# Strassen's seven products for the queries of two heads, with the projection and the keys' transfers moved

## The chip, the core and the metric

The kernel runs on one core of a Trainium2 chip. The metric is device time in microseconds (us) of one launch; less is better. A core has TensorE (PE, matmul; its weight loads are listed as PEld), VectorE (DVE), ScalarE (ACT), GpSimd (POOL) and SyncE (SP), each with a queue of its own that it works off in order, and 16 DMA engines that move data between HBM and on-chip memory. Matmuls write to PSUM, in banks of 128 x 512 floats; the other operands are in SBUF.

## The reference, cut to what matters

All is float32. The input x is 4 batches of 512 rows and 512 columns; a context of 4 x 512 x 256 goes with it. Two layers follow one another; the change is in the second layer's attention, of 16 heads of 128.

```python
# layer 0: attention on the context and a linear map of 4-bit weights
x = x + tanh(g_xattn[0]) * L0_xattn(layernorm(x), ctx)
x = x + tanh(g_ffn[0]) * L0_ffn(layernorm(x))
# layer 1: cross attention, then 16 experts (4 of them for each row of the first batch's 512)
x = x + tanh(g_xattn[1]) * L1_xattn(layernorm(x), ctx)
x = x + tanh(g_ffn[1]) * L1_ffn(layernorm(x))

def L1_xattn(hidden, ctx):
    q = (hidden @ Wq).reshape(B, S, H, D)       # Wq 512 x 2048
    k = (ctx @ Wk).reshape(B, Skv, H, D)        # Wk 256 x 2048
    v = (ctx @ Wv).reshape(B, Skv, H, D)
    q, k = rmsnorm(q, gq), rmsnorm(k, gk)
    attn = softmax(einsum("bqhd,bkhd->bhqk", q, k) / sqrt(D))
    return einsum("bhqk,bkhd->bqhd", attn, v).reshape(B, S, H * D) @ Wo
```

## The kernel before

**Stages.** Layer 0 fills the first 200 us. Layer 1's attention then runs in 32 *groups* m, each one batch and one pair of heads; a group has two *steps* i = 2m + h, one for each head, and each step has four *quarters*, one for each 128 query rows. `step(i)` (L1026) says which pieces are emitted in which quarter. The order of all engines' work is written by hand: `later(n, f)` puts a piece off until n further 512-column matmuls have been emitted, and `tick()` counts one. Each engine gets its instructions in the order of emission, so a piece that is emitted earlier stands ahead of the others on that engine's queue.

**One group.** For group m+1, `keys_values` (8 matmuls of 512 columns, L586) fills keys and values in steps h = 0; ScalarE copies them out of PSUM (L580, L581). The keys are squared (L601), summed on VectorE (L605), scaled on POOL by their inverse root mean square (rk L173, then kn L612), turned in 32x32 blocks on VectorE (L623), and put into the layout of the scores by a round trip to HBM on ScalarE's queue: one transfer out (k_d) and four back (kT, L638), all four at once.

`queries(m+1, h)` runs at h = 1, one head in each of the first two quarters: four matmuls of 512 columns (L660) into one PSUM bank, then ScalarE takes the squares (L666) and the scaled copy qT (L668) straight from PSUM. For both heads, VectorE sums the squares (part, L680), TensorE adds over partitions (L688), VectorE masks and scales (own, L693, and qss, L696), and POOL raises to the power −1/2 (rq, L173).

`scores(i, c)`, one in each quarter, is a matmul (L709) and then on VectorE the row maximum (nmax, L717) and its product with rq (sb, L719), on ScalarE the exponential with its sum (L722), and on VectorE the reciprocal (rden, L726), the division (prob, L727) and the turn of the blocks (tP, L243). With the last quarter `move_probs` issues 16 DMAs on SP (L251), which bring the turned blocks to where `values` needs them (the tile big). `values(i − 2)` is four matmuls (L749) into the single bank psO, copied out by ScalarE (oT, L756). `project` is eight matmuls of a group's two heads with Wo (L776), four pairs, each added to x on VectorE (L258); before the change two pairs run at h = 1 and the other two at the next group's h = 0, in the last quarter.

**Buffers.** PSUM has three banks psA (used by keys_values, queries, project and the experts in turn), two psS (scores), two psT, one psO. The queries' weights wq have two buffers and are loaded two groups ahead, at h = 1's last quarter; `sq` is one buffer that the keys' and the queries' squares share.

**Extra work in some groups.** In groups 11 to 27 (steps 22 to 55) blocks of the experts stand between the pieces (`block_work`, matmuls L853). Groups 4 and 5, 12 and 13, 20 and 21 also normalise and transpose the next batch's rows (`next_rows`), and groups 9 and 10 the rows for the experts (`moe_rows`). In steps 57 to 60 POOL gathers the experts' rows and VectorE adds them back (L258).

Of the kernel before, what the change touches and what calls it, by code (L numbers as in the profile page):

```python
# [9 lines left out]
F32 = mybir.dt.float32  # L10
# [5 lines left out]
P = 128  # L16
# [38 lines left out]
def tile_gated_decoder(  # L55
# [31 lines left out]
    def ps_a():  # L87
        return ps("psA", 3)
# [4 lines left out]
    def ps_t():  # L93
        return ps("psT", 2)
# [7 lines left out]
    def lnt():  # L102
        return work.tile([P, KC, S], F32, tag="lnT", bufs=2, name="lnT")

    def row(tag, bufs):
        return work.tile([P, 512], F32, tag=tag, bufs=bufs, name=tag)

    def col(n, tag):
        return tiny.tile([P, n], F32, tag=tag, name=tag)
# [15 lines left out]
    def load_x(b):  # L125
        nc.sync.dma_start(x_sb[:, b * NC : (b + 1) * NC, :], x_v[:, b * NC : (b + 1) * NC, :])

    wq0 = const.tile([P, CC, D], F32, name="wq0")
    nc.sync.dma_start(wq0, wq0_d.rearrange("(c p) d -> p c d", p=P))
    load_ctx(0)  # L130
    wk0 = const.tile([P, CC, D], F32, name="wk0")
    nc.sync.dma_start(wk0, wk0_d.rearrange("(c p) d -> p c d", p=P))
    small = const.tile([P, NSMALL], F32, name="small")
    nc.sync.dma_start(small, small_d)
# [51 lines left out]
        return mv, rs  # L186

    def normalised(b, c, mv, rs):
        xn = row("xn", 2)
        nc.vector.tensor_scalar(  # L190
            xn, x_sb[:, b * NC + c, :], mv[:, c, 0:1], rs[:, c : c + 1], ALU.subtract, ALU.mult
        )
        return xn
# [168 lines left out]
    def route():  # L362
        def small_tile(shape, tag, dtype=F32):
            return pool0.tile(shape, dtype, tag=tag, bufs=1, name=tag)
# [14 lines left out]
        partf = small_tile([P, 1], "partf")  # L379
        nc.vector.tensor_copy(partf, parti)  # L380

        zero = row("xg", 1)
        nc.gpsimd.memset(zero, 0.0)
        blank = y_d[(NE + SPILL) * P :, :].rearrange("(s p) d -> p s d", p=P)
        nc.gpsimd.dma_start(blank, zero.unsqueeze(1).broadcast_to([P, NSLOT - NE - SPILL, DM]))
# [5 lines left out]
        nc.vector.tensor_copy(idx, topi)  # L391
        idx_v = idx.rearrange("p (c k) -> p c k", k=TOPK)
        ef_b = ef.unsqueeze(1).broadcast_to(CE)
        hit = small_tile([P, TOPK, NC, NE], "hit")
        for k in range(TOPK):
            nc.vector.tensor_tensor(
                hit[:, k], ef_b, idx_v[:, :, k].unsqueeze(2).broadcast_to(CE), ALU.is_equal
# [100 lines left out]
    for c in range(KC):  # L498
        bb = tiny.tile([P, P], F32, tag="bb", bufs=2, name="bb")
        nc.vector.tensor_scalar(bb, ones, bcol[:, c : c + 1], None, ALU.mult)  # L500
        nc.tensor.matmul(pb[:, c * P : (c + 1) * P], bb, ident, start=True, stop=True)
    brow = row("y", 2)
    nc.vector.tensor_copy(brow, pb)

    def linear(b, lx, chunks):
# [22 lines left out]
    GD = G * D  # L528
    groups = [(b, g) for b in range(NB) for g in range(NG)]
    wq_of, wkv_of, wo_of = {}, {}, {}  # L530
    q_of, sq_of, rq_of, kn_of, k_of, v_of, o_of = {}, {}, {}, {}, {}, {}, {}
    turned, moved = {}, {}

    def cols(m):
        g = groups[m][1]
        return slice(g * GD, (g + 1) * GD)

    def load_wkv(m):
# [2 lines left out]
        nc.sync.dma_start(t[:, :, 1, :], wv_v[:, :, cols(m)])  # L541
        wkv_of[m] = t

    def load_wq(m):
        t = work.tile([P, KC, GD], F32, tag="wq", name="wq")
        nc.sync.dma_start(t, wq_v[:, :, cols(m)])
        wq_of[m] = t

    def load_wo(m):
        g = groups[m][1]  # L550
# [9 lines left out]
    def later(n, f):  # L560
        heapq.heappush(pending, (clock[0] + n, next(serial), f))

    def tick(n=1):
        if n == 0:
            return
        clock[0] += n
        while pending and pending[0][0] <= clock[0]:
            heapq.heappop(pending)[2]()

    def keys_values(m, chunks):  # L570
# [61 lines left out]
                st["tK"].rearrange("p j h c q -> p (j h c q)"),  # L632
            )

        def take_in():
            kT = work.tile([P, NT, G, P], F32, tag="kT", name="kT")
            for j in range(NT):
                nc.scalar.dma_start(  # L638
                    kT[j * TB : (j + 1) * TB].rearrange("r t h q -> r t (h q)"),
                    st["k_d"][:, :, j, :].rearrange("t r q -> r t q"),  # L640
                )
            k_of[m] = kT

        later(2, squares)
        later(4, scale)
        later(11, turn)
        later(14, put_out)
        later(18, take_in)

    def queries(m, h):  # L650


        b, wq = groups[m][0], wq_of[m]
        if h == 0:
            sq_of[m] = work.tile([P, G, S], F32, tag="sq", bufs=1, name="sq")
            q_of[m] = []
        sq = sq_of[m]
        pp = ps_a()
        for k in range(KC):
            nc.tensor.matmul(  # L660
                pp, wq[:, k, h * D : (h + 1) * D], lx1[b][:, k, :], start=(k == 0), stop=(k == KC - 1)
            )
            tick()

        def copies():
            nc.scalar.activation(sq[:, h, :], pp, AF.Square)  # L666
            qT = row("qT", 3)
            nc.scalar.activation(qT, pp, AF.Identity, scale=gqk)  # L668
            q_of[m].append(qT)

        later(1, copies)
        if h < G - 1:
            return
        n = G * S // TB
        st = {}

        def part():

            st["part"] = col(n, "part")
            nc.vector.tensor_reduce(  # L680
                st["part"], sq.rearrange("p h (j r) -> p (h j) r", r=TB), AX.X, ALU.add,
                apply_transpose=True,
            )

        def total():

            st["pq"] = ps_t()
            nc.tensor.matmul(st["pq"][:, 0:n], same, st["part"], start=True, stop=True)  # L688

        def scale():  # L690

            own = col(n, "own")
            nc.vector.tensor_tensor(own, st["pq"][:, 0:n], mine, ALU.mult)  # L693
            v = col(G * NC, "qss")
            nc.vector.tensor_reduce(v, own.rearrange("p (c a) -> p c a", a=NT), AX.X, ALU.add)
            nc.vector.tensor_scalar(v, v, 1.0 / D, EPS, ALU.mult, ALU.add)  # L696
            rq_of[m] = col(G * NC, "rq")
            rsqrt(rq_of[m], v, G * NC)

        later(2, part)  # L700
        later(8, total)
        later(9, scale)
# [81 lines left out]
    up_v = up_d.rearrange("e i n -> (e i) n")  # L784
    down_v = down_d.rearrange("e i n -> (e i) n")

    def moe_rows():

        stats = {}

        def chunk(c):
            xn = normalised(0, c, *stats[0])
            later(1, lambda: nc.sync.dma_start(xn_d[c * P : (c + 1) * P, :], xn))

        return [lambda: stats.update({0: layernorm_rows(0)})] + [
            lambda c=c: chunk(c) for c in range(NC)
        ]

    def gather(out, table, k, s):
        nc.gpsimd.indirect_dma_start(  # L800
# [149 lines left out]

    def next_rows(b):

        t = lnt()
        mv, rs = layernorm_rows(b)
        lx1[b] = t
        return [lambda c=c: rows_chunk(t, b, c, mv, rs) for c in range(NC)]

    def rows_chunk(t, b, c, mv, rs):
        xn = normalised(b, c, mv, rs)
        pt = ps_t()  # L960

        def turn():
            for k in range(KC):
                nc.tensor.transpose(pt[:, k * P : (k + 1) * P], xn[:, k * P : (k + 1) * P], ident)

        later(3, turn)
        later(4, lambda: nc.scalar.copy(
            t[:, :, c * P : (c + 1) * P], pt.rearrange("p (k q) -> p k q", k=KC)
        ))

    extra = {}

    def put(i, quarter, *fs):
        extra.setdefault((i, quarter), []).extend(fs)
# [5 lines left out]
    put(4, 3, lambda: load_down(order[0]))  # L980
    for j, f in enumerate(moe_rows()):
        put(first - 3 + j // 4, j % 4, f)
    put(first - 2, 3, lambda: load_rows(order[0]))
    for j, s in enumerate(order):
        for (i, quarter), fs in block_work(s, order[j + 1] if s != order[-1] else None).items():
            put(first + 2 * j + i, quarter, *fs)
# [3 lines left out]
            put(last + 1 + c, k, lambda c=c, k=k: add_row(c, k))  # L990
    for b in range(1, NB):
        i = (b - 1) * NG * G + NG
        chunks = []
        put(i, 3, lambda b=b, chunks=chunks: chunks.extend(next_rows(b)))
        for c in range(NC):
            put(i + 1 + c, 3, lambda c=c, chunks=chunks: chunks[c]())
        if b > 1:
            put(i, 3, lambda b=b: load_ctx(b))

# [1 line left out]


    n, M = G * len(groups), len(groups)
    lxs = [layernorm_T(b) for b in (NB - 2, NB - 1)]
    load_wkv(0)
    load_wq(0)
    load_wkv(1)
    load_wq(1)
    load_wo(0)
    load_wo(1)  # L1010
    keys_values(0, [0, 1, 2, 3])
# [2 lines left out]
    lx1[0] = layernorm_T(0)  # L1014
    keys_values(1, [0, 1, 2, 3])
    tick(30)
    queries(0, 0)
    queries(0, 1)
    tick(30)
    layer0.close()  # L1020
    moe = ctx.enter_context(tc.tile_pool(name="moe", bufs=1))
    for c in range(NC):
# [3 lines left out]
    def step(i):  # L1026
        m, h = divmod(i, G)
        pieces = [[], [], [], []]
        if i >= G:
            pieces[2].append(lambda: values(i - G))  # L1030
        elif h > 0:
            pieces[3].append(lambda: tick(8))
        if h == 0:
            if 0 < m < M - 1:
                pieces[0].append(lambda: keys_values(m + 1, [0, 1]))
                pieces[1].append(lambda: keys_values(m + 1, [2, 3]))
            if m + 2 < M:
                pieces[3].append(lambda: load_wkv(m + 2))
            if m >= 2:
                pieces[3].append(lambda: project(m - 2, [2, 3]))  # L1040
            if 2 <= m < M:
                pieces[3].append(lambda: later(4, lambda: load_wo(m)))
        else:
            if m + 1 < M:
                pieces[0].append(lambda: queries(m + 1, 0))
                pieces[1].append(lambda: queries(m + 1, 1))
            if m + 2 < M:
                pieces[3].append(lambda: load_wq(m + 2))
            if m >= 1:
                pieces[3].append(lambda: project(m - 1, [0, 1] if m < M else [0, 1, 2, 3]))  # L1050
        for quarter in range(4):
            if i < n:
                scores(i, quarter)
            for f in pieces[quarter] + extra.get((i, quarter), []):
                f()

    with tc.manual_schedule():
# [74 lines left out]
```

## Time and profile before

| what | us |
|---|---|
| median of 3 runs | 1508.68 (1507.06 to 1510.2) |
| the profiled execution, its own time | 1506.07 |
| its span, first to last instruction | 1504.3 |
| mean granted TensorE clock in it | 0.985 |
| first scores of group 0 | 211.0 |
| first scores of group 2 | 284.29 |
| first scores of group 11 (nine groups later) | 602.29 |
| first scores of groups 28, 29, 30 | 1330.21, 1374.26, 1411.71 |

The profile comes from one execution. In its rows an instruction is named by engine, line, operation and tiles ("nmax<-psS" reads psS and writes nmax), with its duration and, in brackets, the idle time of its engine just before it and what ended that. A matmul of 512 columns in float32 appears as two records, so a group's 40 matmuls are 80 records (and three small ones). Most of the page's costliest waits belong to engines that have less to do, and cost nothing by themselves:

```profile
L722 ACT ACTIVATE prob<-psS,sb,rq 128x512 f32<-128x512 f32 x256 | 199.2, 778 | 605.3 <-DVE sb L719 582.0
L717 DVE TENSOR_REDUCE nmax<-psS 128x1 f32<-128x512 f32 x256 | 173.0, 676 | 39.5 <-PE psS L709 37.6
L776 PE MATMUL psA<-wo,oT 128*128 128x512 f32 x512 | 238.6, 604 | 11.7 <-ACT oT L756 11.7
```

The first of these rows says that ScalarE's exponentials (256, of 778 ns) were preceded by 605 us of idle time, 582 of it ended by VectorE's sb; the second that VectorE's row maxima were preceded by 39.5 us, mostly ended by the scores' matmul; the third that TensorE waited 11.7 us in the whole run for oT.

### The profile page before, as it was taken

To read this page: it belongs to the slowest core of one execution; us is meant where nothing else is said; L and a number is where in the kernel's file an instruction comes from. 1 tells how busy PE (TensorE), PEld (TensorE's weight loads), DVE (VectorE), ACT (ScalarE), POOL (GpSimd) and SP (SyncE) were. 2 spreads that over 40 slices of the span, in tenths; PEclk is the share of its full clock that TensorE was granted. 3 is DMA by queue.
4 is the path that set the end of the run, shared out by engine and by line. 5 is a ranking of instruction groups with operands and counts; after the bars stand their busy time and mean duration, and the time that the engine had idled before them with its cause. 6 is when DMAs were issued, how large, how long until landed. Compare 5 with 4: busy or idle time off the path is not lost. (4 is left out here: it accounts for less than half of the span.)

```text
span 1504.3 us, 13711 instructions
## 1 busy us (share of the span) xinstructions
PE 1440.6 (96%) x3705; PEld 671.2 (45%) x3705; DVE 961.6 (64%) x2170; ACT 522.1 (35%) x1175; POOL 287.4 (19%) x210
## 2 busy tenths in 40 slices
PE   5899999899999999999999999999999999989987
PEld 2444444344444444444444444444444444434433
DVE  5875537577777777666565655566656655666783
ACT  3521224333343433333333333324333333333331
POOL 2434411221111111111101111112011111112210
PEclk8899999999999999999999999999999999999998
DMA  9610013554444546456665665556656655545643
GB/s 332 231 47 1 15 56 84 151 145 135 126 143 135 147 137 178 117 170 193 174 185 171 184 203 155 174 163 201 184 164 184 184 169 177 171 121 156 182 126 91
DMA packets 156114, 227.93 MB, mean 152 GB/s; under 512 B 24832, under 2 KB 90896, under 8 KB 156032
## 3 DMA queue, kind: packets, MB, share of 16 engines
q1 hardware_dynamic: 128080, 178.91, 40.8%
q10 hardware_dynamic: 23040, 33.56, 7.3%
q0 software_dynamic: 4912, 14.53, 3.4%
q8 instruction: 32, 0.52, 0.1%
q14 instruction: 50, 0.41, 0.1%
HBM read 129.62 MB, written 30.17 MB: 106 GB/s over the span
## 5 line engine op out<-in xcount | busy, mean ns | idle before, releaser
L722 ACT ACTIVATE prob<-psS,sb,rq 128x512 f32<-128x512 f32 x256 | 199.2, 778 | 605.3 <-DVE sb L719 582.0
L709 PE MATMUL psS<-kT,qT 128*128 128x512 f32 x512 | 263.1, 597 | 4.5 <-DMA big<-tP 2.5
L776 PE MATMUL psA<-wo,oT 128*128 128x512 f32 x512 | 238.6, 604 | 11.7 <-ACT oT L756 11.7
L660 PE MATMUL psA<-lnT,wq 128*128 128x512 f32 x512 | 232.9, 596 | 8.2 <-DVEq L894 7.6
L749 PE MATMUL psO<-big,v 128*128 128x512 f32 x512 | 232.8, 598 | 5.2 <-DMA big<-tP 5.2
L586 PE MATMUL psA<-wkv,ctx 128*128 128x512 f32 x512 | 233.5, 596 | 0.2 <-DVE x_sb L258 0.2
L717 DVE TENSOR_REDUCE nmax<-psS 128x1 f32<-128x512 f32 x256 | 173.0, 676 | 39.5 <-PE psS L709 37.6
L243 DVE STREAM_TRANSPOSE tP<-prob 128x512 f32<-128x512 f32 x256 | 181.9, 711 | 9.0 <-DVE prob L727 0.6
L726 DVE RECIPROCAL rden<-den 128x1 f32<-128x1 f32 x256 | 40.6, 159 | 224.6 <-ACT prob L722 219.0
L749 PEld LDWEIGHTS psO<-big,v 128*128 128x128 f32 x512 | 98.1, 192 | 129.6 <-issue 121.7
L776 PEld LDWEIGHTS psA<-wo,oT 128*128 128x128 f32 x512 | 96.9, 193 | 131.0 <-issue 105.4
L660 PEld LDWEIGHTS psA<-lnT,wq 128*128 128x128 f32 x512 | 97.2, 191 | 129.6 <-issue 107.6
L173 POOL TENSOR_TENSOR rq<-qss,mhalf 128x8 f32<-128x8 f32 x32 | 53.3, 1667 | 516.6 <-DVE qss L696 516.6
L258 DVE SCALAR_TENSOR_TENSOR x_sb<-psA,tg,x_sb 128x512 f32<-128x512 f32 x160 | 113.8, 728 | 57.6 <-PE psA L776 21.8
L586 PEld LDWEIGHTS psA<-wkv,ctx 128*128 128x128 f32 x512 | 96.8, 191 | 118.8 <-issue 106.5
L727 DVE TENSOR_SCALAR prob<-prob,rden 128x512 f32<-128x512 f32 x256 | 133.5, 521 | 9.0
L173 POOL TENSOR_TENSOR rk<-kss,mhalf 128x8 f32<-128x8 f32 x32 | 52.5, 1640 | 447.5 <-DVE rden L726 279.8
L709 PEld LDWEIGHTS psS<-kT,qT 128*128 128x128 f32 x512 | 93.2, 191 | 95.6 <-issue 73.2
L853 PE MATMUL psA<-gu,xgT 128*128 128x352 f32 x272 | 86.0, 459 | 0.0
L623 DVE STREAM_TRANSPOSE tK<-kn 128x256 f32<-128x256 f32 x128 | 45.5, 413 | 49.5 <-POOL kn L612 49.5
L853 PEld LDWEIGHTS psA<-gu,xgT 128*128 128x128 f32 x272 | 51.7, 190 | 37.9 <-issue 16.3
L756 ACT COPY oT<-psO 128x512 f32<-128x512 f32 x64 | 37.4, 585 | 77.4 <-PE psO L749 70.2
(157 smaller groups left out, 1283.7 us busy)
## 6 DMA issues: line engine op xcount, KB each, us to landing
big<-tP SPq DMA_DIRECT2D x1024, 64.0 KB
wq<-in_wq_dram SPq DMA_DIRECT2D x32, 512.0 KB
wo<-in_wo_dram SPq DMA_DIRECT2D x32, 512.0 KB
k_d<-tK ACTq DMA_DIRECT2D x32, 512.0 KB
kT<-k_d ACTq DMA_DIRECT2D x128, 128.0 KB
gu<-in_gate_dram SPq DMA_DIRECT2D x16, 704.0 KB
gu<-in_up_dram SPq DMA_DIRECT2D x16, 704.0 KB
wkv<-in_wk_dram SPq DMA_DIRECT2D x32, 256.0 KB
```

The lines of the kernel that those rows point to most:

```text
L173: nc.gpsimd.tensor_tensor(out, v, mhalf[:, :n], ALU.pow)
L243: nc.vector.transpose(tP[:, :, c, :], e.rearrange("p (j r) -> p j r", r=TB))
L258: nc.vector.scalar_tensor_tensor(x_sb[:, t, :], src, gate, x_sb[:, t, :], ALU.mult, ALU.add)
L586: nc.tensor.matmul(pp, ctxs[b][:, k, c * P : (c + 1) * P], wkv[:, k, :, :].rearrange("p a n -> p (a n)"), start=(k == 0), stop=(k == CC - 1),)
L660: nc.tensor.matmul(pp, wq[:, k, h * D : (h + 1) * D], lx1[b][:, k, :], start=(k == 0), stop=(k == KC - 1))
L709: nc.tensor.matmul(sc, q_of[m][h][:, c * P : (c + 1) * P], k_of[m][:, :, h, :], start=True, stop=True)
L717: nc.vector.tensor_reduce(nmax, sc, AX.X, ALU.max, negate=True)
L722: nc.scalar.activation(st["e"], sc, AF.Exp, bias=sb, scale=scale, accum_out=st["den"])
L727: nc.vector.tensor_scalar(st["e"], st["e"], rden, None, ALU.mult)
L749: nc.tensor.matmul(po, v[:, k, h * D : (h + 1) * D], pT[:, :, k, :], start=(k == 0), stop=(k == NC - 1))
L776: nc.tensor.matmul(pp, oT[:, j, c * P : (c + 1) * P], wo[:, j, :], start=(j == 0), stop=(j == G - 1))
L853: nc.tensor.matmul(st[a][:, :FF], st["xgT"][:, k * P : (k + 1) * P], st["gu"][:, a, k, :], start=(k == 0), stop=(k == KC - 1),)
```

## The change

**The queries' product.** For a group, the transposed queries of two heads are a 2 x 2 arrangement of quarters: head by half of the rows (256). Each was the sum of two products, over the halves of the 512 model columns, eight in all. Now there are seven products, by Strassen's scheme in Winograd's form, each two matmuls of 256 columns (14 a group instead of 8 of 512). The sums of quarters of the weights are made once a group on POOL (`combine`), those of the normalised rows once a batch on VectorE (`combine_rows`). The products' sums are made partly by accumulation in PSUM (the first product opens px[:, 0:256] and stays to be added to), partly by five `tensor_tensor` of 128x256 on VectorE and two copies on ScalarE. The squares and the scaled copies (in place) then read SBUF, all four after the last sum.

```diff
     def load_wq(m):
-        t = work.tile([P, KC, GD], F32, tag="wq", name="wq")
-        nc.sync.dma_start(t, wq_v[:, :, cols(m)])
-        wq_of[m] = t
+        w = work.tile([P, KC, GD], F32, tag="wq", bufs=1, name="wq")
+        nc.sync.dma_start(w, wq_v[:, :, cols(m)])
+        sums = work.tile([P, 3, HK, D], F32, tag="wqs", bufs=1, name="wqs")
...
+        def combine():
+            s1, s2, s4 = (sums[:, j] for j in range(3))
+            s3 = quarter(1, 0)
+            nc.gpsimd.tensor_tensor(s1, quarter(1, 0), quarter(1, 1), ALU.add)
+            nc.gpsimd.tensor_tensor(s2, s1, quarter(0, 0), ALU.subtract)
+            nc.gpsimd.tensor_tensor(s3, quarter(0, 0), s3, ALU.subtract)
+            nc.gpsimd.tensor_tensor(s4, quarter(0, 1), s2, ALU.subtract)
+            wq_of[m] = [quarter(0, 0), quarter(0, 1), s4, quarter(1, 1), s1, s2, s3]
+
+        return combine
+
+    def combine_rows(b):
...
+        nc.vector.tensor_tensor(t3, quarter(1, 1), quarter(0, 1), ALU.subtract)
+        nc.vector.tensor_tensor(t1, quarter(0, 1), quarter(0, 0), ALU.subtract)
+        nc.vector.tensor_tensor(t2, quarter(1, 1), t1, ALU.subtract)
+        nc.vector.tensor_tensor(t4, quarter(1, 0), t2, ALU.subtract)
+        lxs_of[b] = [quarter(0, 0), quarter(1, 0), quarter(1, 1), t4, t1, t2, t3]
...
+    def queries(m, part):
...
+        def product(j, out, start):
+            for k in range(HK):
+                nc.tensor.matmul(
+                    out, ws[j][:, k, :], xs[j][:, k, :], start=start and k == 0, stop=k == HK - 1,
+                    skip_group_check=True,
+                )
+                tick(0.5)
+
+        if part == 0:
+            px, py = ps_a(), ps_a()
...
+            def second():
+                nc.scalar.copy(u2, px[:, 0:HS])
+                nc.vector.tensor_tensor(u2, px[:, HS:S], u2, ALU.add)
+
+            def fourth():
+                nc.vector.tensor_tensor(u3, py[:, 0:HS], u2, ALU.add)
+                nc.vector.tensor_tensor(q1[:, HS:S], py[:, HS:S], u3, ALU.add)
+
+            product(0, px[:, 0:HS], True)
+            product(5, px[:, HS:S], False)
+            later(0, second)
+            product(6, py[:, 0:HS], True)
+            product(4, py[:, HS:S], False)
+            later(0, fourth)
             return
...
+        def upper():
+            nc.scalar.copy(q0[:, 0:HS], px[:, 0:HS])
+            nc.vector.tensor_tensor(q1[:, 0:HS], px[:, HS:S], u3, ALU.add)
+
+        def lower():
+            nc.vector.tensor_tensor(q0[:, HS:S], py[:, HS:S], u2, ALU.add)
+            for h in (1, 0):
+                nc.scalar.activation(sq[:, h, :], q_of[m][h], AF.Square)
+            for h in (0, 1):
+                nc.scalar.activation(q_of[m][h], q_of[m][h], AF.Identity, scale=gqk)
+
+        product(1, px[:, 0:HS], False)
+        product(3, px[:, HS:S], True)
+        later(0, upper)
+        product(2, py[:, HS:S], False)
+        later(0, lower)
```

In the changed file these stand at L561 to L564 (combine), L579 to L582 (combine_rows), L693 (the matmuls), L707 and L726 (ScalarE's copies), L708, L711, L712, L727 and L730 (VectorE's sums), L732 and L734 (squares and scaled copies).

**The steps.** Half of the queries moves to the step before, values at h = 1 to the first quarter, and the projection is whole at h = 1; the loads of wkv, wq and wo move along. In quarter 2 of h = 1 the extra work comes ahead of these pieces.

```diff
         if i >= G:
-            pieces[2].append(lambda: values(i - G))
-        elif h > 0:
-            pieces[3].append(lambda: tick(8))
+            pieces[0 if h else 2].append(lambda: values(i - G))
         if h == 0:
...
             if m + 2 < M:
-                pieces[3].append(lambda: load_wkv(m + 2))
-            if m >= 2:
-                pieces[3].append(lambda: project(m - 2, [2, 3]))
-            if 2 <= m < M:
-                pieces[3].append(lambda: later(4, lambda: load_wo(m)))
+                pieces[2].append(lambda: load_wkv(m + 2))
+            if m + 1 < M:
+                pieces[3].append(lambda: queries(m + 1, 0))
         else:
             if m + 1 < M:
-                pieces[0].append(lambda: queries(m + 1, 0))
                 pieces[1].append(lambda: queries(m + 1, 1))
             if m + 2 < M:
-                pieces[3].append(lambda: load_wq(m + 2))
-            if m >= 1:
-                pieces[3].append(lambda: project(m - 1, [0, 1] if m < M else [0, 1, 2, 3]))
+                pieces[2].append(lambda: later(6, load_wq(m + 2)))
+            if m > 0:
+                pieces[2].append(lambda: project(m - 1, [0, 1]))
+                pieces[3].append(lambda: project(m - 1, [2, 3]))
+                if m + 1 < M:
+                    pieces[3].append(lambda: later(2, lambda: load_wo(m + 1)))
+            else:
+                pieces[3].append(lambda: tick(8))
         for quarter in range(4):
...
+            more = extra.get((i, quarter), [])
+            for f in more + pieces[quarter] if h and quarter == 2 else pieces[quarter] + more:
                 f()
```

**The keys' transfers.** The four transfers back are emitted two matmuls apart.

```diff
-        later(14, put_out)
-        later(18, take_in)
+        later(15, put_out)
+        for j in range(NT):
+            later(19 + 2 * j, lambda j=j: take_in(j))
```

**Other moves.** The statistics of the rows are computed one chunk in each quarter instead of four in one (`rows_stats`). combine_rows is emitted two steps before a batch's first, and once in layer 0 ahead of the first queries. In layer 0 `load_wq(0)()` stands ahead of the first rows' normalisation, `load_wq(1)()` behind the first group's queries. Memory for the sums comes from sharing: wq has one buffer instead of two, layer 0's weights lie in the tile of kn, the normalised rows in that of y, and three more tiles changed their tag.

## The prediction

> **What bounds the kernel now.** First the page: the busy times, then the 40 slices.
>
> ```profile
> PE 1440.6 (96%) x3705; PEld 671.2 (45%) x3705; DVE 961.6 (64%) x2170; ACT 522.1 (35%) x1175; POOL 287.4 (19%) x210
> ...
> PE   5899999899999999999999999999999999989987
> ...
> DVE  5875537577777777666565655566656655666783
> ```
>
> TensorE (PE) is full from the fourth slice nearly to the end, so removing matmul columns attacks the right engine on average. An average hides stages. The third view is one group (two heads, two steps) in each of three stages: ahead of the expert blocks, within them, and while experts' rows are added back. The columns after the length are the busy us of PE, PEld, DVE, ACT, POOL.
>
> ```profile
> 479.50:514.00 34.50, 34.50 (x83) 15.38 (x82) 24.64 (x55) 13.36 (x31) 5.17 (x3) 1.00 0.48 137
> 731.00:774.50 43.50, 43.50 (x120) 21.05 (x119) 26.35 (x60) 15.85 (x37) 6.25 (x4) 1.00 0.59 174
> 1374.30:1411.70 37.40, 34.77 (x83) 15.30 (x82) 29.03 (x57) 13.08 (x30) 12.62 (x11) 1.00 0.65 180
> ```
>
> In the first two TensorE never pauses; in the third it does, though its work is nearly that of the first. What is longer there is VectorE (DVE). So the fourth view is VectorE's timeline in the first group: a chunk of scores, the chunk with the queries' squares, and a late chunk.
>
> ```profile
> 482.52 0.68 DVE L717 TENSOR_REDUCE nmax<-psS 128x1 f32<-128x512 f32 x1
> 483.24 0.16 DVE L719 TENSOR_TENSOR sb<-nmax,rq 128x1 f32<-128x1 f32 x1
> 484.33 0.16 DVE L726 RECIPROCAL rden<-den 128x1 f32<-128x1 f32 x1 [0.94 <-ACT prob L722]
> 484.53 0.49 DVE L727 TENSOR_SCALAR prob<-prob,rden 128x512 f32<-128x512 f32 x1
> 485.06 0.71 DVE L243 STREAM_TRANSPOSE tP<-prob 128x512 f32<-128x512 f32 x1
> 485.69 0.65 DVE L717 TENSOR_REDUCE nmax<-psS 128x1 f32<-128x512 f32 x1
> ...
> 489.52 0.16 DVE L719 TENSOR_TENSOR sb<-nmax,rq 128x1 f32<-128x1 f32 x1
> 491.22 1.25 DVE L680 TRANSPOSE_TENSOR_REDUCE part<-sq 128x32 f32<-128x1024 f32 x1 [1.54 <-ACT sq L666]
> 492.55 0.16 DVE L726 RECIPROCAL rden<-den 128x1 f32<-128x1 f32 x1
> ...
> 512.37 1.46 DVE L727 TENSOR_SCALAR prob<-prob,rden 128x512 f32<-128x512 f32 x1
> ```
>
> From nmax to the next nmax is 3.17 us. Of that, 0.94 is idle at rden: the wait for the exponential (L722), which every chunk has. It shows as idle, but the queue cannot use it. So I add VectorE's queue per group with that latency included:
>
> - 8 chunks × 3.17 = 25.4
> - keys' squares reduced: 1.56 (507.68 to 509.76, less the .52 that prob would have taken there)
> - turning the keys, L623: 1.33
> - own and its followers: .40
> - 4 additions to x, L258: .65 each, 2.6
> - part, L680: sb to rden there takes 3.03 with its 1.54 wait, of which .14 would remain without that wait (its 1.24 against the 1.10 of a plain chunk)
> - prob in the last row above: 1.46 instead of .49, +.97. POOL's L612 ran from 511.64 to 513.54.
>
> The sum is **32.4 of 34.56 us** (period of groups 2 to 10: 318.0 us less 7.0 of stalls, over 9). VectorE is 2.1 us from being the bound. The third stretch tests the sum: 32.4 − .97 + 8 additions × .64 + 1.71 (one late sb) + 1.04 (part waits for its squares) = 39.3; nmax to nmax one group later is 39.5. There VectorE sets the pace.
>
> **TensorE's gain.** Before, 8 queries matmuls of 512 columns a group are 16 records; 8 records take 3.43 us.
>
> ```profile
> 479.48 3.60 PE L660 MATMUL psA<-lnT,wq 128*128 128x512 f32 x8
> 482.91 1.02 PE L709 MATMUL psS<-kT,qT 128*128 128x512 f32 x2
> ```
>
> That is .429 each (479.48 to 482.91, eight). Matmuls of 352 columns take .295 each (783.19 to 785.55, eight), in proportion, so 256 take .2145. After: 7 products × 2 × 2 = 28 records × .2145 = 6.00 against 6.86. **−0.86 a group, −27.4 over 32.** Weight loads (190 ns) stay under .2145.
>
> **VectorE's loss.** L666 and L668 read PSUM on ScalarE; afterwards five tensor_tensor of 128x256 on VectorE (L708, L711, L712, L727, L730) and two copies on ScalarE rebuild both heads. Nearest rows, for the price:
>
> ```profile
> L867 DVE TENSOR_TENSOR hh<-hh,psA 128x352 f32<-128x352 f32 x17 | 8.2, 483 | 0.0
> L693 DVE TENSOR_TENSOR own<-psT,mine 128x32 f32<-128x32 f32 x32 | 6.0, 188 | 29.6 <-PE psT L688 29.6
> ```
>
> .92 ns an element between them: 394 ns at 256; start to next start about .31 (.40 at 352). Here the Trainium skill speaks against the change: "VectorE: DVE Perf Modes", on the TRN2 errata, gives fp32 tensor_tensor (N + 151)/0.96 ns, so 424 at 256, and wants tiles of 512 elements or more to spread the fixed part. By rule 5 × .424 = 2.1 us of busy time, by rows 5 × .394 = 2.0; I use the rows. In place:
>
> - L708 and L727 stand between a chunk's sb and rden, where .94 is idle anyway; each wants .40 + .31 − .52, about +.19
> - L711, L712: +.43 and +.31; L730: +.31. With the two above, **+1.43**
> - the squares' chunk: the last tensor_tensor .39, then on ScalarE square .49, square .60, two scalings of .57, and only then the exponential, .91 to rden, since these four are all queued ahead of it. sb to rden is 2.6 at least (part fits in beside) against 1.24 counted above: **+1.35**
> - combine (L561–564): four POOL tensor_tensor of 128x256. POOL's 128x512 row below gives 1380 ns (its shortest 1250), L317's 1024 columns take 2.35 us: 2.15 ns for each further element, so .70 at 256, 2.8 in all, which makes prob or tP wait as in the 1.46 row. The skill's "SBUF — State Buffer" says that a two-port VectorE operation and a GpSimd one share a port pair and the loser blocks fully, so up to 1.4 (two hits); the only row of before shows one hit of .97. With the operations short and mostly beside reductions, I take **+.3**, bounds 0 and 1.4.
>
> ```profile
> L508 POOL TENSOR_TENSOR x_sb<-x_sb,y 128x512 f32<-128x512 f32 x16 | 21.7, 1380 | 23.7 <-DVE xn L190 23.7
> ```
>
> 32.4 + 1.43 + 1.35 + .3 = **35.5 us** (bounds 33.9, where TensorE's 34.56 − .86 = 33.7 nearly binds, and 37). The bound moves from TensorE to VectorE.
>
> **What is moved.** A whole projection at odd steps: same matmuls, same additions; TensorE buffers (two of three psA banks are held by px, py from step h = 0's last quarter to h = 1's second) have their evacuations on VectorE, so its lag reaches TensorE. values(i−2) at h = 1 stands two quarters earlier; its 16 SP transfers (about .62 each, 10.2 a step) are issued the step before, and oT is then ready: a gain where oT was late (5.18 at 273.57 in group 1, 2.6 in the third stretch), else nothing. wo and wkv move past part of SP's 16, with a step in hand. kT's four transfers, now two matmuls apart on ScalarE's queue: the last still leaves four matmuls (3.4 us) and one piece lands in some 2 us: nothing; if late, the first scores of a group wait at most 1 us. Row statistics are spread over quarters: same operations. combine_rows is 4 × about .65 once in each of three groups, and once in layer 0. wq: one buffer, so its DMA is issued after the queries that read it, behind the step's 16 big transfers; it costs nothing while it lands before combine, POOL then needs 2.8 and rq's pow 1.65 must still follow in groups without experts (rival D).
>
> **Sum by stage**, against the profiled execution (1506.07):
>
> - groups 2–10: 9 × 35.5 = 319.5, + row statistics 6.2, xn 3.6, combine_rows 2.6, − 1 hidden = 330.9 against 318.0: **+13**
> - groups 11–27 (42.6 to 43.5 each): VectorE's 33.8 + 3.1 of this change is 36.9, under 42.6, so TensorE's gain comes whole: 17 × .86 = 14.6, less 1 for bank waits: **−13.6**
> - groups 28–30, VectorE's pace already: +2.7 to 3.1 each, **+8**
> - layer 0 and groups 0, 1: half of queries leaves the step of 12.6 us (4 × 3.15, VectorE's pace) for one that TensorE fills, +3.4; the part chunk +1; the 5.18 stall gone, −5; combine between POOL's pow steps in layer 0, +1; together **+1** (−5 to +5)
>
> Total +8.4: 1514.5 in that execution. The runs' median lies 2.6 above the profiled one; so **1517**. A measurement of this kernel can't tell 0.2%, 3 us, from none.
>
> **Rivals.**
>
> - A, the forecast (.58): VectorE sets the pace outside the expert blocks; 1509 to 1530.
> - B, on the other side (.15): TensorE stays the bound everywhere. Price: each group keeps its −.86, and oT stalls go. It needs VectorE's lag under 33.7, that is no port hits and exp's wait absorbed elsewhere. For it: the first stretch, 34.50 of 34.50, and VectorE only 24.64 busy. Against: the 39.3 to 39.5 test. 1508.7 − 27.4 + 1 = about 1482.
> - C (.17): VectorE only breaks even, since ScalarE's queue runs ahead and the squares cost half: a cycle of 34.4, 1.1 less than the forecast's, in 12 groups: 1517 − 13 = about 1504 (1499 to 1507).
> - D (.10): weights late. After 16 big transfers, wq's would land 3.2 to 6.8 us behind its issue (median 4.4 in this trace), combine 2.8, rq 1.64, against about 1 us of slack at the first sb: 1.2 us in 13 groups, 16 on top: about 1533.
>
> **Range and chances.** 1494 to 1531 cuts off most of B and the upper part of D. A's own range is 1509 to 1530. Slower: nearly all of A and D, .62; within 0.2%: A's lower edge and C's upper, .13; faster: B and most of C, .25.
>
> **Right or wrong by the changed profile.** Queries' records .2145 apart. Groups 2–10 with a period of 35 to 36 us and TensorE idle behind a psA bank (released by VectorE) or behind psS's reductions; expert groups 41.8; sb to rden in the squares' chunk 2.6; prob at 1.0 or more beside combine. Wrong if groups 2–10 stay at or under 34.5 with TensorE full (B), or if the first sb of a group waits for POOL's rq (D).

## The result and the profile after

| | median, us | runs | profiled execution (span) |
|---|---|---|---|
| before | 1507.87 | 1505.7 to 1510.2 (4) | 1506.07 (1504.3) |
| after | 1523.3 | 1521.58 to 1525.53 (4) | 1521.58 (1519.8) |

The ratio is 1.0103, 95% interval 1.0081 to 1.0125: the change makes the kernel about 15 us slower. The same rows of the page as before:

```profile
PE 1422.7 (94%) x4089; PEld 744.1 (49%) x4089; DVE 1040.3 (68%) x2346; ACT 547.7 (36%) x1239; POOL 380.7 (25%) x338
...
PE   5799988999899999999999999999999999998886
...
DVE  5876536777777777677667666676677666676873
```

TensorE is busy for 18 us less and the kernel takes 15 us more. VectorE has 79 us more, POOL 93. The slices (38 us each) say where: TensorE is full in the middle, and dips in slices 6, 7 and 11 and over the last four. The windows view puts numbers to it (length, then busy us of PE, PEld, DVE, ACT, POOL), for one group ahead of the expert blocks (group 3), one within them (group 14), one while the experts' rows are added (group 29):

```profile
331.04:367.77 36.73, 34.51 (x95) 17.52 (x94) 26.68 (x60) 14.03 (x33) 8.85 (x9) 1.00 0.46 129
755.40:797.64 42.24, 42.24 (x131) 23.13 (x130) 28.06 (x65) 16.89 (x39) 8.46 (x9) 1.00 0.59 174
1388.39:1429.28 40.89, 34.17 (x91) 17.05 (x90) 32.86 (x69) 14.03 (x33) 15.00 (x15) 0.96 0.64 181
```

Group 14 of before, for comparison:

```profile
732.51:775.57 43.06, 43.06 (x120) 20.83 (x119) 25.91 (x60) 15.85 (x37) 6.25 (x4) 1.00 0.58 171
```

Within the expert blocks TensorE is still busy all the time, and the group is shorter (43.06 to 42.24). In the first window TensorE, which was busy all the time in the one of before, now pauses for 2.2 of 36.7 us. (Group 3 grew by more than most; the mean of groups 2 to 10 is 35.4 us before and 37.3 after.)

The best mark of progress through the whole run is VectorE's row maximum (nmax), the first operation of each of the 256 chunks, since no record of it is missing. Stages from the first nmax of one group to the first nmax of another:

| us | to group 0 | groups 0, 1 | groups 2–10 | groups 11–27 | group 28 to the end | span |
|---|---|---|---|---|---|---|
| before | 217.81 | 67.54 | 318.97 | 727.30 | 172.68 | 1504.3 |
| after | 226.51 | 68.17 | 335.47 | 713.25 | 176.40 | 1519.8 |
| difference | +8.7 | +0.6 | +16.5 | −14.05 | +3.7 | +15.5 |

The chunk with the queries' squares in group 3, on VectorE's timeline, answers to the one shown of before:

```profile
354.88 0.16 DVE L793 RECIPROCAL rden<-den 128x1 f32<-128x1 f32 x1 [0.94 <-ACT prob L789]
355.07 0.49 DVE L794 TENSOR_SCALAR prob<-prob,rden 128x512 f32<-128x512 f32 x1
355.47 0.42 DVE L727 TENSOR_TENSOR qT<-psA,u 128x256 f32<-128x256 f32 x1
355.81 0.70 DVE L243 STREAM_TRANSPOSE tP<-prob 128x512 f32<-128x512 f32 x1
356.43 0.39 DVE L730 TENSOR_TENSOR qT<-psA,u 128x256 f32<-128x256 f32 x1
356.74 0.68 DVE L784 TENSOR_REDUCE nmax<-psS 128x1 f32<-128x512 f32 x1
357.45 0.16 DVE L786 TENSOR_TENSOR sb<-nmax,rq 128x1 f32<-128x1 f32 x1
357.57 1.25 DVE L747 TRANSPOSE_TENSOR_REDUCE part<-sq 128x32 f32<-128x1024 f32 x1
359.70 0.17 DVE L793 RECIPROCAL rden<-den 128x1 f32<-128x1 f32 x1 [0.88 <-ACT prob L789]
```

VectorE works without a gap but for the wait that every chunk has. From sb to rden it is 2.25 us here (1.10 in a plain chunk), because the exponential is queued behind two squares and two scalings on ScalarE:

```profile
356.91 0.63 ACT L732 ACTIVATE sq<-qT 128x512 f32<-128x512 f32 x1 [0.36 <-DVE qT L730]
357.57 0.72 ACT L734 ACTIVATE qT<-qT,gqk 128x512 f32<-128x512 f32 x1
358.20 0.71 ACT L734 ACTIVATE qT<-qT,gqk 128x512 f32<-128x512 f32 x1
358.81 0.76 ACT L789 ACTIVATE prob<-psS,sb,rq 128x512 f32<-128x512 f32 x1
```

Over groups 2 to 10 VectorE waited for the scores' matmul 9.48 us before and 1.43 us after. TensorE now waits for VectorE there, mostly for banks psA that VectorE has still to empty. The longest of its waits in these groups, first of before, then of after (us in total, times, longest):

```profile
PE psA L776 <- ACT oT L756: 2.1, 2, 1.6
```

```profile
PE psA L843 <- DVE x_sb L258: 8.9, 9, 1.8
PE psA L843 <- DVE qT L727: 4.3, 4, 1.4
PE psA L622 <- DVE x_sb L258: 3.8, 5, 0.9
```

VectorE had become the engine that the others wait for.

One row stands for a wait that the forecast's sum did not have. At the start of group 3:

```profile
331.04 0.67 DVE L784 TENSOR_REDUCE nmax<-psS 128x1 f32<-128x512 f32 x1
333.02 0.16 DVE L786 TENSOR_TENSOR sb<-nmax,rq 128x1 f32<-128x1 f32 x1 [1.31 <-POOL rq L173]
```

and the same moment on POOL's timeline:

```profile
328.46 0.72 POOL L561 TENSOR_TENSOR wqs<-wq 128x256 f32<-128x256 f32 x1 [14.65 <-DMA wq<-in_wq_dram]
329.26 0.73 POOL L562 TENSOR_TENSOR wqs<-wqs,wq 128x256 f32<-128x256 f32 x1
329.94 0.73 POOL L563 TENSOR_TENSOR wq<-wq 128x256 f32<-128x256 f32 x1
330.63 0.73 POOL L564 TENSOR_TENSOR wqs<-wq,wqs 128x256 f32<-128x256 f32 x1
331.31 1.68 POOL L173 TENSOR_TENSOR rq<-qss,mhalf 128x8 f32<-128x8 f32 x1
```

combine waits for its weights, takes 2.85 us, and rq's power, whose input stood ready at 329.2, comes behind it. The waits view counts 10.3 us of sb waiting for rq on VectorE in the whole run, 7 times (before: 1.2 us, once).

### The profile page after: what moved, and what is told of

Read it like the earlier page. It is cut to its first block, busy times and chain, and to the rows that moved or that the text cites. A ratio compares the mean times of both kernels' runs of the same rounds, so it can differ in the third digit from the quotient of the medians.

```text
span 1519.8 us, 14979 instructions
## 1 busy us (share of the span) xinstructions
PE 1422.7 (94%) x4089; PEld 744.1 (49%) x4089; DVE 1040.3 (68%) x2346; ACT 547.7 (36%) x1239; POOL 380.7 (25%) x338
## 5 line engine op out<-in xcount | busy, mean ns | idle before, releaser
L776 PE MATMUL psS<-kT,qT 128*128 128x512 f32 x512 | 267.3, 605 | 16.4 <-ACT prob L789 5.2
L561 POOL TENSOR_TENSOR wqs<-wq 128x256 f32<-128x256 f32 x32 | 23.3, 727 | 222.7 <-DMA wq<-in_wq_dram 176.0
L693 PE MATMUL psA<-lnT,wq 128*128 128x256 f32 x256 | 65.8, 379 | 0.0
L693 PE MATMUL psA<-lxs,wq 128*128 128x256 f32 x256 | 65.7, 379 | 0.0
```

The costliest lines, as they stand in the source:

```text
L693: nc.tensor.matmul(out, ws[j][:, k, :], xs[j][:, k, :], start=start and k == 0, stop=k == HK - 1, skip_group_check=True,)
L776: nc.tensor.matmul(sc, q_of[m][h][:, c * P : (c + 1) * P], k_of[m][:, :, h, :], start=True, stop=True)
```

## The experiments

All runs compare with the kernel before on the same chip (1507 to 1508 us); after is 1523.3.

**e1, combine behind rq.** Nothing but POOL's order changes.

```diff
-                pieces[2].append(lambda: later(6, load_wq(m + 2)))
+                pieces[2].append(lambda: later(12, load_wq(m + 2)))
```

> Only POOL's four combine operations move, from ahead of rq's power to behind it (12 matmuls after the step's third quarter begins instead of 6). Theory (VectorE sets the pace outside the expert blocks, and part of its loss is that sb waits for rq behind combine; in the changed kernel sb waits 10.3 us in all for rq, 7 times): those waits go and the time falls by 7 to 11 us, to 1512 to 1516. Rival (these waits are slack: what counts is that two of three psA banks are held by the queries, or the sums themselves): 1520 to 1524.

Measured 1516.95 us, ratio 1.0065 (1.0046 to 1.0084): 6.3 us off, just outside the expected 7 to 11 and far from the rival. The waits for rq fell from 10.3 us to 1.2. Of the 16.5 us that groups 2 to 10 had lost, 2.8 came back (335.47 to 332.69), and 2.1 in groups 0 and 1; so most of the loss lies elsewhere.

**e2, scalings behind the exponential.**

```diff
             for h in (1, 0):
                 nc.scalar.activation(sq[:, h, :], q_of[m][h], AF.Square)
-            for h in (0, 1):
-                nc.scalar.activation(q_of[m][h], q_of[m][h], AF.Identity, scale=gqk)
+            later(2, scaled)
+
+        def scaled():
+            for h in (0, 1):
+                nc.scalar.activation(q_of[m][h], q_of[m][h], AF.Identity, scale=gqk)
```

> Only ScalarE's two scalings of the queries move, behind the exponential of the chunk with the squares. Theory (VectorE's pace): sb to rden in that chunk falls from 2.25 to about 1.4 us, .85 in each of some 14 groups outside the expert blocks, 12 us off: about 1511. Rival (TensorE waits on held banks, VectorE has room): 1520 to 1524.

In this run the scaling of the very first group comes behind its first chunk of scores, which therefore uses unscaled queries; no operation is left out. In the profiled execution layer 0 gets 8.6 us shorter by this, and groups 0 and 1 get 7.1 longer. Measured 1521.19 us, ratio 1.0094 (1.0074 to 1.0113): 2 us off where 12 were expected, and hardly clear of noise. (The runs lie at 1517.9 to 1522.3, those of after at 1521.6 to 1525.5.) VectorE's timeline of group 3 says why. The chunk with the squares did what it should:

```profile
357.63 0.16 DVE L789 TENSOR_TENSOR sb<-nmax,rq 128x1 f32<-128x1 f32 x1
357.75 1.25 DVE L750 TRANSPOSE_TENSOR_REDUCE part<-sq 128x32 f32<-128x1024 f32 x1
358.92 0.12 DVE L796 RECIPROCAL rden<-den 128x1 f32<-128x1 f32 x1
...
366.36 0.68 DVE L787 TENSOR_REDUCE nmax<-psS 128x1 f32<-128x512 f32 x1
368.95 0.16 DVE L789 TENSOR_TENSOR sb<-nmax,rq 128x1 f32<-128x1 f32 x1 [1.92 <-POOL rq L173]
```

sb to rden is 1.29 instead of 2.25, and the next group's first sb waits 1.92 us for rq. Over groups 2 to 10 part and the wait behind it took 7.9 us less, the waits for rq rose from 3.6 to 10.8, and the groups were only 2.9 us shorter. The gain was made and then spent waiting for POOL, which e1 had just shown to be removable. So the two belong together.

**e3, first group plain.** Group 0's queries by eight products of 512 columns; no combine in layer 0.

```diff
-    combine_rows(0)
     queries(0, 0)
     queries(0, 1)
...
+    put(0, 1, lambda: combine_rows(0))
```

> The first group's queries by eight products of 512 columns as before, so without combine in layer 0 and with combine_rows(0) in step 0 instead of ahead of the first queries. Theory: layer 0 gets back the 2.85 us of combine's blocking at 60 to 72 us and the 5.16 us that the first scores waited for the sums' chain, less .86 of TensorE: first row maximum 6 to 8 us earlier, the total 1515 to 1517. Rival (the delay is only handed on, since VectorE is as full afterwards): under 3 us, 1520 to 1523.

Measured 1518.79 us, ratio 1.0078 (1.0057 to 1.0099): 4.5 us off, short of the 6 to 8. The first nmax came 6.75 us earlier (226.51 to 219.76), but groups 0 and 1 took 2.4 us more, so part was handed on. Two rows show what the first scores had waited for: TensorE, then VectorE, of the changed kernel.

```profile
218.44 2.07 PE L776 MATMUL psS<-kT,qT 128*128 128x512 f32 x2 [5.16 <-ACT qT L734]
```

```profile
214.16 1.42 DVE L659 STREAM_TRANSPOSE tK<-kn 128x256 f32<-128x256 f32 x4 [2.65 <-POOL kn L648]
215.51 0.39 DVE L727 TENSOR_TENSOR qT<-psA,u 128x256 f32<-128x256 f32 x1
```

The last products were done at 213.3; their sums stood on VectorE behind the keys' turn, which waited for POOL, and behind the sums came four operations of ScalarE. In steady groups work fills that chain; ahead of the first scores nothing does. Of the 2.85 us that layer 0 lost earlier, only .9 went with combine (the last transposes of rows came at 200.95 in after, 200.06 here, 198.11 before).

**e4, the moves alone.** All queries plain, nothing of Strassen, everything else of the change kept.

```diff
     def queries(m, part):
-        ws, xs = wq_of[m], lxs_of[groups[m][0]]
+        plain_queries(m, part)
+        return
...
-        put(b * NG * G - 2, 1, lambda b=b: combine_rows(b))
```

> All queries by eight products of 512 columns, squares and scaled copies from PSUM as before, no combine and no combine_rows; everything else of the change (half of the queries a step earlier, the whole projection in odd steps, values, the loads, the keys' transfers spread, one buffer for wq) stays. Theory (the products' sums on VectorE and their followers are the loss, the moves cost nothing): 1503 to 1509, like before or a little under. Rival (the moved pieces and transfers, one wq buffer, banks): 1515 or more.

Measured 1501.73 us, ratio 0.9962 (0.9951 to 0.9973), faster than before. So the seven products, with the moves in place, cost 1523.3 − 1501.7 = 21.6 us, and the moves gain 6.5. By stages, after takes 7.0 us more than e4 up to group 0, 6.7 in groups 0 and 1, 18.8 in groups 2 to 10, 13.6 less in groups 11 to 27, and 3.6 more from group 28 on. The window of group 3, by the columns named above, is TensorE's again:

```profile
315.70:350.12 34.42, 34.42 (x83) 15.36 (x82) 24.70 (x55) 13.81 (x31) 5.17 (x3) 1.00 0.49 138
```

**e5, the three edits together.** e1, e2 (with the first group scaled at once) and e3.

> The edits of e1, e2 and e3 together (combine behind rq; scalings behind the exponential, except in the first group; the first group's queries plain), seven products in all other groups. In e2 the chunk with the squares lost its .87 us and sb's wait for rq grew from 3.6 to 10.8 us in groups 2 to 10. Theory (one queue, VectorE's, and POOL's rq right behind it): with combine out of the way e2's gain appears, so the three add up to more than singly: 1523.3 less 6 (e1), less 4 (e3), less .87 x 13 = 11 and nothing back: about 1501, 1498 to 1505. Rival (e2's gain is lost to another limit than rq, say TensorE's banks): 1510 or more.

Measured 1507.75 us, ratio 1.000 (0.9989 to 1.0011). Singly the edits had given 6.3, 2.1 and 4.5, together 15.6. That is more than the 12.9 of their sum, as the theory says, but the 2.7 between them are not clear of noise; clearer are groups 2 to 10 of the profiles, where e1 gave 2.8 us, e2 2.9 and e5 8.3. The total is 3 us short of the theory's range. VectorE's wait for rq is gone (0.6 us in all), but in groups 2 to 10 it now waits 5.7 us for the scores' matmuls, where it had waited 1.4, so TensorE is close behind. Part of that may be the spread transfers, since TensorE now waits for kT at the first scores of five groups:

```profile
PE psS L814 <- DMA kT<-k_d: 7.2, 5, 3.5
```

In after this was 2.5 us, in e4 nothing. How much of the missing 3 us it explains, no run separates. Groups 2 to 10 take 327.1 us, against 316.6 in e4. The sums themselves remain: from their starts to the next ones they hold VectorE's queue for 15.7 us there, while prob and the turn of the blocks, ahead of them, hold it 3.3 less.

**e6, sums twice.** Four of the five VectorE sums are made twice, with the same result.

```diff
                 nc.vector.tensor_tensor(u3, py[:, 0:HS], u2, ALU.add)
+                nc.vector.tensor_tensor(u3, py[:, 0:HS], u2, ALU.add)
...
             nc.vector.tensor_tensor(q1[:, 0:HS], px[:, HS:S], u3, ALU.add)
+            nc.vector.tensor_tensor(q1[:, 0:HS], px[:, HS:S], u3, ALU.add)
```

> Four of the five VectorE sums of each group are made twice (same operands, same result), .33 each, 1.3 us of VectorE in every group; nothing else. Theory (VectorE sets the pace outside the expert blocks and has room within them): groups 2 to 10 and 28 to 31 grow by 1.0 to 1.3 us each, groups 12 to 27 by under .1; the total 1533 to 1541. Rival (TensorE or held banks set the pace): under 4 us in all, or as much in the expert groups as outside.

Measured 1548.98 us, ratio 1.0277 (1.0253 to 1.03): 25.7 us more, above the expected range, on the theory's side. Groups 2 to 10 grew by 13.5 us (335.47 to 348.95), 1.5 each; the seventeen groups 11 to 27 by 3.1 in all; from group 28 on by 6.1; layer 0 and the first two groups by 5.5. The size was off since a sum whose result the next instruction reads or writes over took .41 to .46 to the next start, the others .31 to .34; the doubled ones stand in the first case. In groups 2 to 10 they put 16.5 us into VectorE's queue, .46 each, and its 3.6 us of waits for rq went, so what was added is paid almost whole. In groups 11 to 27 they put 31 us into the queue, and 3.1 were paid. The rival, held banks or TensorE, is out.

**e7, keys at once.** The keys' four transfers back as before the change.

```diff
-        later(15, put_out)
-        for j in range(NT):
-            later(19 + 2 * j, lambda j=j: take_in(j))
+        later(14, put_out)
+        for j in range(NT):
+            later(18, lambda j=j: take_in(j))
```

> The keys' transfers as before the change (out 14 matmuls behind, all four back 18 behind). Theory (spreading costs nothing but the 2.3 us that TensorE waited for kT in group 29): 1520 to 1524. Rival (it holds up the first scores, or relieves ScalarE's queue): more than 4 us either way.

Measured 1560.37 us, ratio 1.0355 (1.0329 to 1.0381): 37 us slower than after. My theory here was wrong by all of it. On ScalarE's timeline of group 5, its queue's DMA issues among it:

```profile
402.05 0.85 ACTq L674 DMA_DIRECT2D kT<-k_d  x2
...
403.41 1.66 ACTq L674 DMA_DIRECT2D kT<-k_d  x2
405.11 0.37 ACT L726 COPY qT<-psA 128x256 f32<-128x256 f32 x1 [2.33 <-DMA big<-tP]
```

and on VectorE's:

```profile
405.52 0.42 DVE L727 TENSOR_TENSOR qT<-psA,u 128x256 f32<-128x256 f32 x1 [2.02 <-ACT qT L726]
```

ScalarE issues the four transfers in a row from 402.05, and until the last is issued at 405.1 nothing that stands behind them starts. The four issues themselves take .31 to .48, 1.4 us in all, so about half of these 3 us is waiting, for which the profile gives no cause. Its small copy L726 stands behind them, the sum L727 waits for the copy, and all of VectorE's queue waits behind L727. The waits view counts 33.4 us of L727 for L726 in 13 places: 4.2 in groups 0 and 1, 19.6 in groups 2 to 10, 9.6 from group 28 on, where the profiled execution lost 4.5, 17.5 and 8.8. In groups 11 to 27, which lost 6.9, L727 never waits; there VectorE's rden waits 27 us more for the exponentials. (The releaser in the first bracket, big, is inferred; what ends at that moment on ScalarE's own queue is the issue of the last transfer.) In the changed kernel one transfer is issued ahead of the copy and the others behind it.

**e9, the same with plain queries.** e4 and e7's edit.

> e4 (all queries plain, the moves kept) with the keys' four transfers at once as in e7. Theory (e7 lost 37 us because ScalarE's copy L726, behind the transfers that wait for the keys' way out, holds up a sum on VectorE, 2.2 us in each group; the plain queries have no VectorE work there but part): at most 5 us over e4's 1501.7, 1501 to 1507. Rival (the waiting transfers stop the exponentials and so VectorE whatever the queries are): 1520 or more.

Measured 1508.53 us, ratio 1.0011 (1.0000 to 1.0023): 6.8 us over e4, a little more than the 5 allowed, and nowhere near the rival's. The spreading is worth 37 us to the seven products and 7 to plain queries. There VectorE's part waits for the squares behind the transfers (8.9 us in groups 2 to 10, none in e4). It also means that the other moves (halves of the queries, values, the whole projection, loads) come to nothing in sum: e9 equals before within 0.2%.

**e8, seven products only in groups 12 to 28**, whose queries run while expert blocks are woven in; the others plain. In the last batch VectorE restores the one quarter of the rows that combine_rows overwrote.

```diff
+    plain = [m for m in range(len(groups)) if not 12 <= m <= 28]
...
+        put({1: G * 12 - 2}.get(b, b * NG * G - 2), 1, lambda b=b: combine_rows(b))
+        if b == 1:
+            put(G * 28 - 1, 3, lambda: restore_rows(NB - 1))
```

> Seven products only for groups 12 to 28, whose queries run while expert blocks are woven in; the other groups' queries plain as in e4 (its 1501.7 is the measure); the last batch's rows are restored by one VectorE addition after group 28. Theory (the seven products gain .83 us where TensorE is the bound and lose where VectorE is): 1501.7 - 17 x .83 = 1487.6, 1485 to 1491. Rival (the gain in expert groups needs the state that the other groups leave, or plain groups behind them fall further behind): 1494 or more.

Measured 1489.11 us, ratio 0.9878 (0.985 to 0.9906), inside the expected range: faster than before and after. One of its expert groups:

```profile
723.41:765.66 42.25, 42.25 (x131) 23.13 (x130) 28.06 (x64) 16.89 (x39) 8.75 (x9) 1.00 0.57 175
```

TensorE has no gap and VectorE is busy for 28 of 42 us.

**e10, e8 with the edits of e1 and e2.**

> e8 with combine behind rq and the scalings behind the exponential. Theory (in the expert groups TensorE is the bound and VectorE has room, so what it saves there is worth nothing): 1487 to 1491, as e8. Rival (these waits cost in expert groups too): 1485 or less.

Measured 1489.91 us, ratio 0.9886 (0.9869 to 0.9902), the same as e8. Groups 11 to 27 take 713.4 us in it and 713.6 in e8: what VectorE or POOL saves there is worth nothing.

## Why the prediction was right or wrong

Forecast 1517 with a range of 1494 to 1531; measured 1523.3. The direction and the mechanism (VectorE sets the pace outside the expert blocks, TensorE within them) held. One of the prediction's own signs of being wrong came too: the first sb of a group waits for rq (D). On the profiled executions the sum said +8.4; it was +15.5. That the total is off by no more is partly luck: layer 0 with groups 0 and 1 came out 8.3 too low and groups 2 to 10 by 3.6, while the end of the run was forecast 4.3 too high and the expert groups .45.

- **TensorE's gain: right.** Two rows of the TensorE timeline of after, four records to a row, stand .86 apart, .215 each:

```profile
529.10 1.03 PE L693 MATMUL psA<-lnT,wq 128*128 128x256 f32 x4
529.96 1.03 PE L693 MATMUL psA<-lxs,wqs 128*128 128x256 f32 x4
```

  The page's busy time fell by 18 us, not by 27.4: 14.0 of them in groups 11 to 27, where TensorE never pauses, and only 1.5 in groups 2 to 10, where it now does. What keeps the busy time up beside the pauses stays open.

- **Expert groups: right.** −13.6 forecast, −14.05 measured; e8 and e10 show that neither VectorE nor POOL counts there.
- **Groups 2–10: right in mechanism, short by 3.6.** +13 forecast, +16.5 measured. The five sums came to what was forecast. The prediction's words put L708 and L727 between a chunk's sb and rden, where the exponential's wait would cover them; they stand behind prob. But its sum, .40 + .31 − .52, is that of the true place: from prob to tP it is .74 with one of them between (the rows of group 3 above) and .53 without, so .21 each where .19 was taken. L711, L712 and L730 take .43, .34 and .31, as forecast but for .03. The squares' chunk is 2.16 on the mean of the nine, not 2.6, so 4.0 us too much were taken. What the sum had put at nothing is more than that: sb's wait for rq, 3.6 us; one wait of 1.7 for a buffer of the normalised rows, which now share y's two; 1.4 of waits for the scores that stayed.
- **The wait for rq was rival D's.** It came as D drew it: wq landed 3.9 to 7.6 us behind its issue (3.2 to 6.8 were forecast), combine took 2.85 (2.8) and the power 1.68 (1.64). But D was a separate case of .10 with a price of 16 us, where the wait was a term of A: 3.6 us in these groups and 10.3 in the run, 9.1 more than before.
- **The price of a sum: right.** The prediction took 394 ns from the rows of before; by the formula of the Trainium skill ("VectorE: DVE Perf Modes", on the TRN2 errata) it would be 424 for 256 elements, an estimate, since the page has it measured at 512 and 2048. By form, of after:

```profile
L708 DVE TENSOR_TENSOR u<-psA,u 128x256 f32<-128x256 f32 x32 | 13.3, 416 | 0.0
```

  The five rows lie between 386 and 425, so both were near. What counts in the queue is the distance to the next start, .31 to .45.
- **combine's hits: right.** The Trainium skill ("SBUF — State Buffer", on who interferes with whom) has a two-port VectorE operation and a GpSimd one share a port pair, and the later of them blocked. The trace agrees: VectorE's prob takes .49 alone and up to 1.03 beside combine's additions. Over nine groups these cost 1.9 us on prob and 1.1 on the scaling of qss, .33 a group where .3 was taken. e1 did not remove them; behind rq, combine hit sb instead, for 3.1 us.
- **Layer 0 and groups 0, 1: wrong, and the largest miss.** +1 forecast, +9.3 measured. The step summed +3.4, +1, −5 (the stall of 5.18 gone) and +1 for combine. It left out that group 0's scores follow the queries at once, so that the chain of sums, squares and scalings lies bare: 5.16 us. combine ahead of them cost .9 (e3). And the stall of 5.18 did go, but another took its place, which VectorE's timeline shows in group 1:

```profile
260.52 0.16 DVE L786 TENSOR_TENSOR sb<-nmax,rq 128x1 f32<-128x1 f32 x1 [5.09 <-POOL rq L173]
```

  In e4, without combine and the sums, the first two groups take 61.43 us, 6.1 less than before, so the moves gave what the step expected of them and more; in after they take 68.17.
- **From group 28 on: too high.** +8 forecast, +3.7 measured. Groups 28 to 30 were priced at +2.7 to 3.1 each, as if VectorE's load were all the pace there. In group 28 it was not: VectorE had waited 9.8 us for the scores before, waits 1.0 after, and the group grew by only .3. Groups 29 and 30 grew by 1.4 and 1.7 (39.49 to 40.89, 36.83 to 38.52); in group 29 the chunk with the squares had already waited for them before, by 1.04.
- **The spread transfers, "nothing": wrong in reason.** The step asked only whether kT would come late for the scores. It didn't ask what stands behind a transfer's issue on ScalarE. The spread hides 37 us of e7's loss, and e4 shows a gain of 6.5 without the products. It did make kT late, by 2.31 us at the first scores of group 30, where the step allowed 1 us at most.

Rival B asked for −27; the gain is there only in the expert groups. Rival C's point, that VectorE breaks even, is about what e5 reaches, after three edits.

## What to carry to other kernels

Work taken from the busiest engine is worth something only in stages where no other engine is close behind it: sum each engine's queue per stage, unavoidable waits included, and apply such a change only where the other queue has room, as e8 does. When operations are added to a queue, look at what stands next behind them, including short ones: 2.9 us of preparation ahead of a power of eight columns made VectorE wait, and DMAs issued in a row hold up everything behind them on the issuing engine. A saving that does not show may have turned into the next wait; pair the edits before judging one (in groups 2 to 10 e1 and e2 alone gave 2.8 and 2.9 us, with e3 8.3).

## What was not expected of the hardware

In layer 0 the kernels without combine there (e3, e4, e8) still lose 1.95, 1.66 and .92 us up to the last transposes of rows. The trace points to the order of two engines; no run tested it alone. VectorE's L324 took .74 before and 2.40 after, because POOL's L317 (2.35 us) started .5 earlier than it, at 55.22, and VectorE stood until it ended. Before, L324 had started first, and POOL took 2.87. Which of the two waits seems decided by a few tenths of a microsecond upstream; e3, e4 and e8 show the long L324 too (2.50, 2.72, 2.61).

Of after:

```profile
55.22 2.35 POOL L317 TENSOR_TENSOR pw<-pw,nw 128x1024 f32<-128x1024 f32 x1 [1.52 <-ACT pw L315]
55.72 2.40 DVE L324 SCALAR_TENSOR_TENSOR w<-pw,em,w 128x512 f32<-128x512 f32 x1
```

Of before:

```profile
55.44 0.74 DVE L324 SCALAR_TENSOR_TENSOR w<-pw,em,w 128x512 f32<-128x512 f32 x1
55.53 2.87 POOL L317 TENSOR_TENSOR pw<-pw,nw 128x1024 f32<-128x1024 f32 x1 [2.12 <-ACT pw L315]
```
